# Dummy matmuls in the beginning of a two-layer cross-attention kernel

## The chip, the cores and the metric

The kernel runs on one core of a Trainium2 chip. A core has five engines with their own instruction queues: TensorE (PE: matmuls, with its weight loads shown apart as PEld), VectorE (DVE), ScalarE (ACT), GpSimd (POOL) and SyncE (SP, which here only starts DMA transfers). Each engine works through its queue in order and waits for the others by semaphores. The metric is the device time of one execution in microseconds (us), the median of the runs.

## What is computed

Two cross-attention layers, one after the other, on x (16 items, 256 rows, 320 channels) with a context of 16 x 256 x 512. There are 20 heads of 16 channels. The first layer, cut to what matters:

```python
text = context[:, :77]; ip = context[:, 77:]        # 77 text tokens, 179 image tokens
q = x @ Wq
text_out = softmax(q_h @ k_h.T * scale) @ v_h       # per head, keys and values from text
scores   = q_h @ ip_k_h.T * scale                   # per head, keys from ip
text_probs = softmax(q @ k_text.T * scale)          # over all channels, not per head
sem   = (text_probs @ text) @ ip.T * scale          # one row of image scores for all heads
ip_out = softmax(scores + 0.5 * sem) * mask @ ip_v_h
x = (text_out + ip_out) @ Wout + bout + x
```

The second layer has the same form with 252 text and 4 image tokens and a normalised semantic term per head. All arithmetic must be near f32.

## The kernel before

**Products.** PE multiplies in a rounded 32-bit format (`fp32r`), so each operand is split into a rounded high part (a cast on ACT) and a low remainder (a subtraction on DVE or POOL): `halves`. A product is then three matmuls for each 128 rows of contraction (high by high, high by low, low by high): `prod`. Results go to PSUM; a PSUM bank holds 128 x 512 f32. The general banks are called X; `bank()` hands out three of them in turn (`BANKS`, `"X": 3`), so a product waits until what stood in the bank three products earlier has been read.

**The two layers as slots.** An item's 20 heads are five groups of four, so each layer has 80 slots, numbered k. For a group, `stacks0(k)` loads by DMA a stacked query matrix `qs` and key matrix `ks` (parts Q and K: the query and key rows out of DRAM, where `queries` and `keys_out` wrote them, to `qd` and `kd`; parts T and M: the text probabilities `tph` and a Gram matrix `M` of the context), `score0` multiplies them into the S banks and takes row maxima on DVE, `maxima0` turns the maxima by a matmul with the identity `ident_r` and loads them into the stack, `turned0` multiplies again, transposed, into the T banks and takes exponentials on ACT and a factor on POOL, `attend0` multiplies by the values. `slot0(k)` lists that work for a slot, with marks (`yield 0.2`, `yield 0.6`) at which other tasks that are due are filled in.

**The beginning.** Before slot 0 nothing is there to overlap with. The loads and splits of the context, of the weights and of x stand first in the program (`all_halves`); then `begin()` runs single steps of the tasks of items 0 and 1 by hand: `k0` is the keys of both items (weights `wA` for the text keys, `wB` for the rest), `q0` the queries (split of x into `hq`, three products with `wE`), `m0t` the Gram matrix, `s0` the semantic term (products of `kb` and `q`, softmax, two transposes, products of `tph` and `M`), `v0` the values (`wC`, `wD`). `begin()` fixes the order on all five engines, the loop over slots only that of PE; the loads and splits ahead of `begin()` and, in the loop, the work of the other engines are placed by the scheduler of the framework, so that a change on PE can move them.

A line that the steps below need: `nc.vector.tensor_scalar_mul(wqt[:, 2, ...], ..., tmask[:, 3:4])` (L308) masks the low part of the last rows of `wE`, and the query products that use them come after it. `zone` is a 128 x 32 f32 tile of zeroes with a column of ones, `hsn` an f32 tile of 128 x 768 that collects attention results.

Of the kernel before, what the change touches and what calls it, by code (L numbers as in the profile page):

```python
# [49 lines left out]
def xattn2(  # L50
# [27 lines left out]
    nc = tc.nc  # L78
    f = lambda ap: ap.bitcast(F32)
    mm = nc.tensor.matmul  # L80
# [9 lines left out]
    def bank(tag="X"):  # L90
        return ps.tile([128, 512], F32, tag=tag, name=tag, bufs=BANKS[tag])
# [4 lines left out]
    def own(tag):  # L96

        n, *ring = kept[tag]
        kept[tag][0] += 1
        return ring[n % len(ring)]  # L100

    def scores(kept=False):

        s = whole if kept else ps.tile([128, 1024], F32, tag="S", name="S", bufs=1)
        return s.rearrange("p (h t) -> p h t", h=4)
# [4 lines left out]
    def buf(tag, shape, dtype=F32, bufs=1, name=None):  # L110
        if tag in ("wB", "wD", "vr", "raw"):
            return sb.tile(shape, dtype, tag=tag, name=name or tag, bufs=bufs)
        size = 1
        for d in shape[1:]:
            size *= d
        if tag not in slots:
            slots[tag] = [0, dtype] + [const_tile([128, max(size, words.get(tag, 0))], f"{tag}_{i}", dtype) for i in range(bufs)]
        n, kind, *ring = slots[tag]
        assert kind == dtype and len(ring) == bufs, tag
        slots[tag][0] += 1  # L120
        t = ring[n % bufs][: shape[0], :size]
        names = "abcd"[: len(shape) - 1]
        if len(names) > 1:
            t = t.rearrange(f"p ({' '.join(names)}) -> p {' '.join(names)}", **dict(zip(names, shape[1:])))
        return t

    def const_tile(shape, tag, dtype=F32):
        return const.tile(shape, dtype, tag=tag, name=tag)
# [7 lines left out]
    ident_r = const_tile([128, 128], "ident_r", FR)  # L136
# [6 lines left out]
    def queued(inst, *behind):  # L143

        for other in behind or [anchors.get(inst.ins.engine)]:
            if other is not None:
                tc.add_manual_dep(
                    inst.ins, other.ins.name, mybir.DependencyInfo(mybir.DependencyClass.NoSync, mybir.DependencyReason.DATA), reason="order"
                )
        return inst  # L150

    def anchor(inst):
        anchors[inst.ins.engine] = inst
        return inst
# [186 lines left out]
    zone = const_tile([128, 32], "zone")  # L341
    nc.vector.memset(zone, 0.0)
    nc.vector.memset(zone[:, 21:22], 1.0)
    hsn = const_tile([128, 3, 8, 2, 16], "hsn")
    nc.gpsimd.memset(f(buf("q", [128, 2, 3, S], FR))[64:, :, 2], 0.0)

    rn = const_tile([128, BI], "rn")
# [296 lines left out]
    def load(src, tag):  # L644
        x = buf(tag, [128, 3, S])
        dma(x, src.rearrange("(k p) t -> p k t", p=128))
        return x
# [59 lines left out]
    def stacks0(k, parts="KQTM"):  # L707
        b, g = divmod(k, NG)
        Q, K = QK[k] = qs[k % SIZES["NR"]], ks[k % SIZES["NR"]]
        for part in parts:  # L710
            if part == "K":
                dma(K[0:XROW], stack_rows(kd[0][b // 2][:, :, b % 2], g))
            elif part == "Q":
                dma(Q[0:XROW], stack_rows(get("q0", b)[1], g))
            elif g < SIZES["NR"]:
                tph, mh = get("s0", b)[1::2] if part == "T" else (None, get("m0t", b))
                if part == "T":
                    dma(Q[XROW : XROW + T0], tph[:, 0:1].to_broadcast([T0, 4, S]))
                else:
                    dma(K[XROW : XROW + T0, :, T0:], mh[:, 0:1, T0:].to_broadcast([T0, 4, S - T0]))  # L720
# [19 lines left out]
    def score0(k, t):  # L740
        Q, K = QK[k]
        if t == 0:
            maxes[k] = buf("mn", [128, 2, 2, 4], FR, bufs=2)
        mn = maxes[k]
        sp = scores(True)
        for h in range(4):
            mm(sp[:, h], Q[: XROW + T0, h, t * 128 : (t + 1) * 128], K[: XROW + T0, h], start=True, stop=True)  # L747
        nc.vector.tensor_reduce(mn[:, t, 0], sp[:, :, :T0], axis=AX.X, op=ALU.max)  # L748
        anchor(nc.vector.tensor_reduce(mn[:, t, 1], sp[:, :, T0:], axis=AX.X, op=ALU.max))  # L749

    def maxima0(k, queue=nc.scalar):
        Q, mn = QK[k][0], maxes[k]
        mp = bank()
        for t in range(2):
            mm(mp[:8, t * 128 : (t + 1) * 128], mn[:, t].rearrange("p a h -> p (a h)"), ident_r, start=True, stop=True)
        mt = buf("mt", [8, S], FR)
        nc.scalar.copy(mt, mp[:8, :S])  # L757
        for a in range(2):
            row = XROW + T0 + a
            issues[k] = queue.dma_start(f(Q[row : row + 1]), f(mt[4 * a : 4 * a + 4]))  # L760

    def turned0(k, t):

        rs = get("s0", k // NG)[2]
        Q, K = QK[k]
        for p in range(2):
            if t == 0:
                P[k, p] = buf("P", [128, 2, 2, S], bufs=SIZES["NP"])
        st = [own("T").rearrange("p (h t) -> p h t", h=2) for p in range(2)]
        for p in range(2):  # L770
            for j in range(2):
                mm(st[p][:, j], K[:KS0, 2 * p + j, t * 128 : (t + 1) * 128], Q[:KS0, 2 * p + j], start=True, stop=True)  # L772
        for p in range(2):
            pt = P[k, p][:, t]
            exp = anchor(nc.scalar.activation(pt, st[p], AF.Exp, scale=SCALE))  # L775
            if t and k + 1 in issues:
                queued(exp, issues[k + 1])
            anchor(nc.gpsimd.tensor_mul(pt, pt, rs[:, t : t + 1].to_broadcast([128, 2, S])))  # L778

    def attend0(k):  # L780
        b, g = divmod(k, NG)
        v, pv = get("v0", b), own("P")
        for vt in range(3):
            values0(k, pv, v, vt)
        settle0(b, g, pv)

    def slot0(k):
        if k > 0:
            yield lambda: maxima(k + 1)
        yield lambda: ahead(k + 2, 0)  # L790
        yield lambda: turned0(k, 0)
        yield 0.2
        if k > 0:
            yield lambda: attend0(k - 1)
        yield lambda: ahead(k + 2, 1)
        yield lambda: turned0(k, 1)
        yield lambda: stacks(k + LEAD)
        yield 0.6
        yield 1.0

# [328 lines left out]
    def step(key):  # L1129
        t = tasks[key]  # L1130
        if callable(t[2]):
            for n in t[3]:
                get(*n)
            t[2] = t[2]()
        try:
            next(t[2])
            t[1] += 1
        except StopIteration as e:
            results[key] = e.value
            del tasks[key]  # L1140

    def get(*key):
        while key not in results:
            step(key)
        return results[key]
# [27 lines left out]
    for c in range(B // 2):  # L1173
        n, k = 10 * c, [("k0", c)] if c else []
# [11 lines left out]
    for b in range(B):  # L1186
        n = NS + 5 * b
# [17 lines left out]
    def stacks(k):  # L1205
        if 0 <= k < 2 * NS:
            (stacks0 if k < NS else stacks1)(k)

    def ahead(k, t):
        if k < NS:  # L1210
            score0(k, t)
        else:
            both1(k - 2, t)

    def maxima(k):
        if k < 2 * NS:
            (maxima0 if k < NS else maxima1)(k)

    def begin():
        parts = lambda *keys: [step(key) for key in keys if key in tasks]  # L1220
        k0, q0, s0, m0, q1 = ("k0", 0), ("q0", 0), ("s0", 0), ("m0t", 0), ("q0", 1)
        parts(k0, k0, k0, q0, q0, q1, q0, q0, q0)
        get(*q0)
        get(*m0)
        parts(s0, s0, s0, s0, s0)
        stacks0(0, "M")
        stacks0(1, "M")
        parts(k0, k0, k0, s0, q1, q1, q1, q1)
        stacks0(0, "QK")
        get(*s0)  # L1230
        stacks0(0, "T")
        stacks0(1, "QKT")
        get("v0", 0)
        v1 = ("v0", 1)
        stacks0(2)
        parts(k0)
        score0(0, 0)
        parts(v1)
        score0(0, 1)
        get("m0t", 1)  # L1240
        maxima0(0, nc.sync)
        parts(v1)
        get(*v1)
        get(*q1)
        score0(1, 0)
        stacks0(3)
        score0(1, 1)
        parts(*[("s0", 1)] * 3)
        maxima0(1, nc.sync)
        parts(("s0", 1), ("s0", 1), ("k0", 1))  # L1250
        resid0.append(load(xT_d[0], "xc"))
        dma(mk, mk_d)
        dma(bo[:, 0, :], bo0_d)
        dma(bo[:, 1, :], bo1_d)
        fill(-1e-6)
# [93 lines left out]
```

## Time and profile before

| what | us |
|---|---|
| runs | 1521.59, 1528.58, 5161.13 |
| median of the runs | 1528.58 |
| the profiled execution | 1527.85 |
| its span, first to last instruction | 1526.1 |
| PE busy, share of the span | 1432.1 (94%) |
| DVE, ACT, POOL busy | 1125.5 (74%), 920.5 (60%), 1219.6 (80%) |

One run is far off the other two; the median is not moved by it. The page also cuts the span into 40 slices of 38 us and gives for each the busy share of an engine in tenths and the clock that PE was granted:

```profile
PE   6789999999999999789999999999999999999996
PEclk9899999999999998889999999999999999999997
```

PE is nearly always busy, but for the first two slices, a place in the middle where the second layer begins, and the end; in the same places the granted clock is under full. How such views are read: a group or a piece of timeline has its start and length in us, the engine, the line of the program, the operation, what it writes and reads, and in square brackets the idle time before it and what ended that. A matmul's length contains a latency that overlaps with the next, so the cost of matmuls in a row is read from start to start.

### The profile page before, as it was taken

The page shows a single profiled execution, that of the slowest core. Times are in us where ns is not written, and L with a number is a line of the kernel's source. Part 1 is how long each engine was busy: PE and PEld are TensorE (multiplying, and loading weights), DVE is VectorE, ACT ScalarE, POOL GpSimd, SP SyncE. Part 2 cuts the span into 40 slices and gives each one's busy share as a digit, 9 for nine tenths or more (in the row PEclk, how much of TensorE's full clock was granted, in tenths as well). Part 3 has the DMA queues.
Part 4 walks back from the last instruction along what each step waited for, and adds up shares of the span by engine and source line. Part 5 has one row for each costly group of instructions (what it writes and reads, how often), then busy time and mean ns, then how long its engine had stood idle before and what let it go on. Part 6 is the DMA issues. An engine that isn't in the chain of part 4 may idle for free.

```text
span 1526.1 us, 36176 instructions
## 1 busy us (share of the span) xinstructions
PE 1432.1 (94%) x12678; PEld 1158.5 (76%) x12678; DVE 1125.5 (74%) x2546; ACT 920.5 (60%) x2168; POOL 1219.6 (80%) x1583
## 2 busy tenths in 40 slices
PE   6789999999999999789999999999999999999996
PEld 6678878888888877667777777777777777777764
DVE  5467767676767677877777878887878778787884
ACT  5346565656555644556666766667756666677562
POOL 4269898989898976789678888788878788888785
PEclk9899999999999998889999999999999999999997
DMA  6766776767767664676354344444444344433311
GB/s 205 203 190 194 219 195 213 200 210 203 214 181 218 190 200 125 187 210 183 104 142 123 110 121 129 126 121 134 112 116 144 112 112 135 135 114 99 109 30 40
DMA packets 228753, 232.95 MB, mean 153 GB/s; under 512 B 38298, under 2 KB 198460, under 8 KB 228572
## 3 DMA queue, kind: packets, MB, share of 16 engines
q1 hardware_dynamic: 226364, 229.34, 52.2%
q8 instruction: 101, 1.65, 0.5%
q10 hardware_dynamic: 2208, 1.30, 0.4%
q14 instruction: 80, 0.66, 0.2%
HBM read 117.65 MB, written 77.20 MB: 128 GB/s over the span
## 4 chain that ended last, share of the span: by engine, by line
PE 67%; DMA 10%; POOL 8%; DVE 6%; ACT 3%; issue 2%; SPq 2%; ACTq 1%; POOLq 0%; DVEq 0%
PE X L946 13%; PE X L248 13%; PE X L614 6%; PE P L805 6%; PE S L747 5%; PE P L958 4%; PE P L968 4%; PE T L772 3%; PE S L903 3%; POOL wt L937 3%; PE T L897 3%; SPq L83 2%; DMA rawc<-in_cT_dram 2%; PE X L617 2%; PE X L573 2%
## 5 line engine op out<-in xcount | busy, mean ns | idle before, releaser
L778 POOL TENSOR_TENSOR P<-P,rs 128x512 f32<-128x512 f32 x320 | 408.9, 1304 | 103.1 <-ACT P L775 102.7
L937 POOL TENSOR_TENSOR wt<-P,ctb 128x512 f32<-128x512 f32 x320 | 406.4, 1293 | 57.5 <-ACT ctb L936 57.5
L946 PE MATMUL X<-ctb,gm 128*128 128x512 f32 x1120 | 301.5, 401 | 2.4 <-DVE wt L947 2.4
L775 ACT ACTIVATE P<-T 128x512 f32<-128x512 f32 x320 | 176.0, 595 | 155.9 <-PE T L772 126.0
L947 DVE TENSOR_TENSOR wt<-X,wt 128x512 f32<-128x512 f32 x320 | 217.5, 683 | 58.2 <-PE X L946 55.0
L946 PEld LDWEIGHTS X<-ctb,gm 128*128 128x128 f32 x1120 | 194.7, 189 | 41.6 <-DVE wt L947 12.0
L917 ACT ACTIVATE P<-T 128x512 f32<-128x512 f32 x320 | 174.5, 592 | 80.4 <-PE T L897 77.4
L936 ACT ACTIVATE ctb<-P 128x512 fp32r<-128x512 f32 x320 | 184.3, 626 | 12.8 <-PE X L946 9.9
L905 DVE TENSOR_REDUCE mn<-S 128x4 fp32r<-128x1008 f32 x160 | 191.2, 1195 | 0.0
L749 DVE TENSOR_REDUCE mn<-S 128x4 fp32r<-128x716 f32 x160 | 142.5, 891 | 0.0
L805 PE MATMUL P<-P,vr 128*32 128x256 f32 x1920 | 127.7, 396 | 4.5 <-POOL P L778 2.3
L747 PE MATMUL S<-ks,qs 125*128 125x256 f32 x640 | 118.2, 308 | 8.3 <-DMA qs<-tph 4.6
L747 PEld LDWEIGHTS S<-ks,qs 125*128 125x128 f32 x640 | 89.0, 195 | 43.7 <-issue 29.2
L772 PE MATMUL T<-qs,ks 127*128 127x256 f32 x640 | 106.7, 290 | 2.4 <-ACT P L775 1.3
L748 DVE TENSOR_REDUCE mn<-S 128x4 fp32r<-128x308 f32 x160 | 74.7, 467 | 34.0 <-PE S L747 33.2
L772 PEld LDWEIGHTS T<-qs,ks 127*128 127x128 f32 x640 | 90.8, 195 | 3.9 <-ACT P L775 1.7
L805 PEld LDWEIGHTS P<-P,vr 128*32 128x32 f32 x1920 | 56.7, 112 | 47.0 <-issue 7.0
L816 DVE STREAM_TRANSPOSE nt<-P 128x512 f32<-128x512 f32 x80 | 56.9, 712 | 45.3 <-PE P L805 44.3
L958 PE MATMUL P<-P,v1t 128*32 128x256 f32 x1280 | 85.7, 385 | 0.0
L968 PE MATMUL P<-wt,zone 128*32 128x256 f32 x1280 | 84.4, 379 | 0.3 <-DVE wt L947 0.3
L614 PE MATMUL X<-hq,wE 128*128 128x256 f32 x512 | 77.7, 296 | 7.2 <-ACT hq L601 3.9
L614 PE MATMUL X<-ho,wF 128*128 128x256 f32 x512 | 76.3, 292 | 7.2 <-ACT mt L757 3.7
(249 smaller groups left out, 3022.3 us busy)
## 6 DMA issues: line engine op xcount, KB each, us to landing
qd<-q SPq DMA_DIRECT2D x96, 256.0 KB
qs<-tph SPq DMA_DIRECT2D x64, 308.0 KB
rawc<-in_cT_dram SPq DMA_DIRECT2D x60, 256.0 KB
qs<-qd SPq DMA_DIRECT2D x80, 192.0 KB
ks<-kd SPq DMA_DIRECT2D x80, 192.0 KB
ks<-kd SPq DMA_DIRECT2D x160, 96.0 KB
qs<-qd SPq DMA_DIRECT2D x160, 96.0 KB
kd<-kst SPq DMA_DIRECT2D x57, 256.0 KB
```

What stands on the lines that cost most here:

```text
L248: last = mm(out, lhs(a, k), rhs(b, k), start=i == 0, stop=i == len(terms) - 1)
L614: mm(pp, w(s, k, m), a[:, t], start=i == 0, stop=i == len(terms) - 1)
L747: mm(sp[:, h], Q[: XROW + T0, h, t * 128 : (t + 1) * 128], K[: XROW + T0, h], start=True, stop=True)
L772: mm(st[p][:, j], K[:KS0, 2 * p + j, t * 128 : (t + 1) * 128], Q[:KS0, 2 * p + j], start=True, stop=True)
L775: exp = anchor(nc.scalar.activation(pt, st[p], AF.Exp, scale=SCALE))
L778: anchor(nc.gpsimd.tensor_mul(pt, pt, rs[:, t : t + 1].to_broadcast([128, 2, S])))
L805: mm(pv[32 * s : 32 * s + 32, o : o + S], v[:, vt, h : h + 32], P[k, s // 2][:, t, s % 2], start=vt < 2, stop=vt != 1,)
L905: anchor(nc.vector.tensor_reduce(maxes[k + 2][:, t], sp[:, :, :T1], axis=AX.X, op=ALU.max))
L936: nc.scalar.activation(R[k, u][:, t], P[k, u][:, t], AF.Copy, scale=0.5)
L937: anchor(nc.gpsimd.tensor_sub(W[k, u][:, t], P[k, u][:, t], f(R[k, u][:, t])))
L946: mm(yp, gm[:, gb], R[k, u][:, kt], start=i == 0, stop=i == len(blocks[n]) - 1)
L947: w1["wt"] = nc.vector.tensor_mul(W[k, u][:, n], yp, W[k, u][:, n])
```

## The change

The change adds matmuls whose results nobody reads, in six places, and a memset:

- `hsn` is set to zero by DVE at the start;
- five f32 matmuls of `zone` with the zeroes of `hsn` at the head of `begin()` (four of 256 columns, one of 128);
- a function `warm(n)`: n matmuls of the identity with itself repeated, 128 x 512, into one X bank;
- `warm(10)` before the queries of item 0, `warm(6)` before those of item 1, `warm(16)` before the first score, and `warm(7)` twice in slot 0: before the second item's transposes and before its `tph` products.

```diff
     hsn = const_tile([128, 3, 8, 2, 16], "hsn")
+    nc.vector.memset(hsn, 0.0)
...
         yield lambda: turned0(k, 0)
+        if k == 0:
+            yield lambda: warm(7)
         yield 0.2
...
         yield lambda: stacks(k + LEAD)
+        if k == 0:
+            yield lambda: warm(7)
         yield 0.6
...
+    def warm(n):
+
+        out = bank()
+        for i in range(n):
+            mm(out, ident_r, ident_r.unsqueeze(1).to_broadcast([128, 4, 128]), start=True, stop=True)
+
     def begin():
+        out = bank()
+        for m, half in ((0, slice(0, 8)), (1, slice(0, 8)), (2, slice(0, 4))):
+            rhs = hsn[:, m, half].rearrange("p f r d -> p (f r d)")
+            for i in range(2 if m < 2 else 1):
+                mm(out[:32, : rhs.shape[1]], zone, rhs, start=True, stop=True)
...
-        parts(k0, k0, k0, q0, q0, q1, q0, q0, q0)
+        parts(k0, k0, k0, q0, q0, q1)
+        warm(10)
+        parts(q0, q0, q0)
...
-        parts(k0, k0, k0, s0, q1, q1, q1, q1)
+        parts(k0, k0, k0, s0, q1)
+        warm(6)
+        parts(q1, q1, q1)
...
         parts(k0)
+        warm(16)
         score0(0, 0)
```

The scheduler also places some loads and splits of the beginning otherwise. On ACT, from the first evacuation of key products (`kst`) to the split of x (`hq`), there stands before (the names: `wB`, `wC`, `wE` are weights that are split, `raw`, `rawc` and `P` the buffers they were loaded into, `ho` the third key tile):

```order
L160 CAST kst_0_254<-X_259 128x2x77
L160 CAST wB_90<-P_1_97 128x320
L160 CAST wE_0_88<-raw_137 128x320
L160 CAST wB_91<-P_2_98 128x320
L160 CAST wC_0_172<-raw_176 128x320
L160 CAST kst_1_255<-X_275 128x2x77
L160 CAST wB_92<-P_3_99 128x320
L160 CAST wC_0_172<-rawc_0_93 128x320
L267 CAST ho_0_256<-X_291 64x2x77
L268 COPY both_0_300<-X_291 64x154
L601 CAST hq_0_307<-xq_0_133 128x512
L602 ACTIVATE hq_0_307<-xq_0_133,tmask_81 128x256
```

and now:

```order
L160 CAST kst_0_261<-X_266 128x2x77
L160 CAST wB_89<-P_0_96 128x320
L160 CAST wB_90<-P_1_97 128x320
L160 CAST kst_1_262<-X_282 128x2x77
L267 CAST ho_0_263<-X_298 64x2x77
L268 COPY both_0_307<-X_298 64x154
L602 CAST hq_0_314<-xq_0_133 128x512
L603 ACTIVATE hq_0_314<-xq_0_133,tmask_81 128x256
L160 CAST wE_0_88<-raw_137 128x320
L160 CAST wB_91<-P_2_98 128x320
L160 CAST wC_0_172<-raw_176 128x320
L160 CAST wB_92<-P_3_99 128x320
```

All three key evacuations and the split of x have moved ahead of five weight splits, which now wait behind what PE has to deliver.

On DVE the low parts follow the same way. After the split of x, up to the mask of `wE` (L308), there stands now:

```order
L604 TENSOR_TENSOR hq_0_314<-xq_0_133,hq_0_314 128x512
L605 TENSOR_TENSOR hq_0_314<-xq_0_133,hq_0_314 128x256
L163 TENSOR_TENSOR wE_0_88<-raw_137,wE_0_88 128x260
L163 TENSOR_TENSOR wE_0_88<-raw_137,wE_0_88 128x4
L163 TENSOR_TENSOR wE_0_88<-raw_137,wE_0_88 128x60
L163 TENSOR_TENSOR wB_91<-P_2_98,wB_91 128x260
L163 TENSOR_TENSOR wB_91<-P_2_98,wB_91 128x4
L163 TENSOR_TENSOR wB_91<-P_2_98,wB_91 128x60
L163 TENSOR_TENSOR wC_0_172<-raw_176,wC_0_172 128x320
```

followed by `wB_92` (three rows), `wC_0_172` and L308; before, L308 stood ahead of `wB_92` and of the split of x.

On PE, at the first score (S; `wC` and `wD` are the value products around it, `ident_r` the identity), the difference is:

```order
 L248 MATMUL X<-wD,ctb_85 128x320 x3
 L248 MATMUL X<-wD,ctb_86 128x320 x3
-L747 MATMUL S<-ks_207,qs_203 128x256 x4
+L1228 MATMUL X<-ident_r 128x512 x16
+L748 MATMUL S<-ks_207,qs_203 128x256 x4
 L248 MATMUL X<-wC_172,cta_83 128x320 x3
 L248 MATMUL X<-wC_172,cta_84 128x320 x3
```

Nothing is moved here; the sixteen stand between the values of item 0 and the score. After slot 0 the order on PE is unchanged, on SP and POOL it differs in a few places by one or two rows, and on DVE and ACT in some dozens of places of the first layer by one to seven rows.

## The prediction

> **What bounds the kernel now.** I read the windows first. Columns: stretch, length, busy time and instruction count of PE, PEld, DVE, ACT, POOL, then granted clock, DMA share, GB/s.
>
> ```profile
> 0.00:35.50 35.50, 23.05 (x112) 21.05 (x112) 22.29 (x81) 20.74 (x52) 16.75 (x25) 1.00 0.67 210
> 35.50:38.90 3.40, 3.06 (x14) 3.07 (x15) 0.42 (x1) 0.37 (x1) 1.14 (x3) 0.50 0.72 187
> 38.90:49.20 10.30, 6.70 (x48) 6.43 (x46) 1.27 (x3) 3.21 (x7) 0.23 (x1) 1.00 0.78 211
> 49.20:56.00 6.80, 5.81 (x25) 5.84 (x26) 1.81 (x4) 0.53 (x1) 0.00 (x0) 0.50 0.90 267
> 69.60:76.30 6.70, 4.76 (x22) 4.51 (x23) 5.72 (x9) 4.74 (x10) 4.95 (x4) 0.50 0.92 241
> 110.00:290.00 180.00, 175.66 (x1666) 152.47 (x1660) 125.66 (x300) 106.92 (x253) 163.03 (x158) 1.00 0.69 198
> 290.00:740.00 450.00, 412.71 (x3734) 346.14 (x3734) 322.41 (x754) 250.27 (x595) 377.72 (x384) 0.94 0.67 193
> ```
>
> From 110 to 290 us PE is busy 175.66 of 180 us: what the beginning saves reaches the end nearly one for one. The beginning is another regime: three stretches (35.5 to 38.9, 49.2 to 56.0, 69.6 to 76.3) run at half clock, 3.4, 6.8 and 6.7 us long, as if the clock were set once in 3.4 us. The first row says 1.00, but there the rate of the matmuls, from the PE timeline, is the better witness (start, length, engine, line, operation, count):
>
> ```profile
> 10.85 1.49 PE L248 MATMUL X<-cta,wA 128*128 128x156 f32 x6
> 12.13 1.49 PE L248 MATMUL X<-ctb,wA 128*128 128x156 f32 x6
> 81.42 0.79 PE L248 MATMUL X<-cta,wA 128*128 128x156 f32 x6
> 82.05 0.83 PE L248 MATMUL X<-ctb,wA 128*128 128x156 f32 x6
> 22.45 1.27 PE L617 MATMUL X<-hq,wE 128*128 128x256 f32 x5
> 35.84 3.42 PE L614 MATMUL X<-hq,wE 128*128 128x256 f32 x15 [0.97 <-POOL hq L603]
> 39.09 0.75 PE L617 MATMUL X<-hq,wE 128*128 128x256 f32 x5
> 39.68 0.28 PE L698 MATMUL X<-tph,M 77*128 77x256 f32 x1
> ```
>
> Start to start, six key products take 12.13-10.85 = 1.28 us (0.213 each) early and 0.63 us (0.105) at 81 us. The query product costs (39.09-35.84)/15 = 0.217 us at 36 us, where half clock is recorded, and (39.68-39.09)/5 = 0.118 after it; at 22.45 five take 1.27 us against 0.75. So PE is at half rate through its early work too.
>
> How much work holds the clock? Busy PE in single windows of 3.4 us laid on the same grid:
>
> ```profile
> 49.20:52.60 3.40, 2.41 (x10) 0.50 0.84 216
> 59.40:62.80 3.40, 2.02 (x15) 1.00 0.44 126
> 66.20:69.60 3.40, 1.63 (x10) 1.00 0.54 151
> ```
>
> After 2.02 us of work (59%) full clock stayed; after 1.63 us (48%) it fell. After 2.41 us (71%) it was not given back; after 3.06 us (90%, second row of all) it was. [...]
>
> **The change, part by part.** The price of a dummy, at full clock:
>
> ```profile
> 905.27 1.05 PE L968 MATMUL P<-wt,zone 128*32 128x256 f32 x16
> ```
>
> A 128x512 identity product streams twice the columns of a 128x256 one: 2x0.118 = 0.236 us (an estimate), 0.47 at half clock. The products on zeroes are f32 like this zone group: 16 records, two for each product and four products side by side, in 1.05 us, so one product takes about 0.5 us, the block of four and a half 2.3, and 4.6 at half clock. It waits for the added hsn memset, which no row shows; a POOL memset of 1024 elements takes 0.96 us (below), so 768 take about 0.7, hidden since DVE has nothing before 4.80 us. The zeroes run from 1.8 to 6.4 us against a first product at 5.18 that in any case waits for its splits until 7.02: cost 0.
>
> ```profile
> 0.88 0.96 POOL L326 MEMSET ks<- 128x1024 f32 x1
> 4.80 0.69 DVE L163 TENSOR_TENSOR cta<-rawc,cta 128x512 fp32r<-128x512 f32 x1 [3.78 <-ACT cta L160]
> 7.02 0.96 PE L248 MATMUL X<-cta,wA 128*128 128x156 f32 x3 [0.63 <-ACT wA L160]
> 14.81 0.62 DVE L163 TENSOR_TENSOR wB<-P,wB 128x260 fp32r<-128x260 f32 x3
> 15.50 0.46 ACT L160 CAST wB<-P 128x320 fp32r<-128x320 f32 x1 [0.96 <-DMA P<-in_wki_dram]
> 16.28 0.38 DVE L308 TENSOR_SCALAR wE<-wE,tmask 128x320 fp32r<-128x320 f32 x1
> 26.29 1.01 PE L670 MATMUL X<-kb,q 128*128 128x156 f32 x7 [0.21 <-DVE q L270]
> ```
>
> Term 1, up to the semantic products of item 0 at 26.29. ACT's order now has the key evacuations and the split of x ahead of the splits of wE row 2 and wB; POOL's order is as before. If PE had full clock from 10.85, the remaining 20 key products end near 10.85+20x0.105 = 13, and ACT's four evacuations and the split of x, each some 0.4 us, near 15. DVE subtracts from 14.2 on, once half of x is cast, seven groups of about 0.6 us like the wB one, before it comes to L308: 18.4 (the last wB load, landed at 15.50, is no limit then). The 14 query products that need L308 end near 21 at the latest, against 22.45+1.27 = 23.7 at half clock now: about 2.6 us early. If PE stays at half, the keys end at 15.2 as now, ACT stands idle for them, L308 slips from 16.28 to 20.8, and 14 products of 0.217 end at 23.8: 0. I expect something between. The zeroes fill a window and release the clock; but then three products at 0.105 per load of some 1.5 us are far under 48% busy, so it falls again before 10.85 and returns inside the unbroken run that follows, between 12.6 and 15. That is nearer the low end: 1.2 us. The ten identity products after the keys (2.4 to 4.7 us) end before L308 in either case: 0.
>
> Term 2, queries of item 1. Six dummies (1.4 us) fill most of the 1.71 us gap before 34.48; with the 0.4 us product there and what ran before, the window stays near 59%. Fifteen products then take 15x0.118 = 1.8 us instead of 39.09-35.84 = 3.25: 1.5 us, on the chain, since SP's row of writes to qd and then the stack loads follow them:
>
> ```profile
> 34.48 0.39 PE L614 MATMUL X<-hq,wE 128*128 128x256 f32 x1 [1.71 <-ACT hq L601]
> 44.21 5.85 DMA qs<-tph
> 50.19 1.19 PE L747 MATMUL S<-ks,qs 125*128 125x256 f32 x4 [4.59 <-DMA qs<-tph]
> 51.19 1.80 PE L248 MATMUL X<-wC,cta 128*128 128x320 f32 x6
> 54.38 1.05 PE L747 MATMUL S<-ks,qs 125*128 125x256 f32 x4
> 55.24 1.04 PE L248 MATMUL X<-cta 128*77 128x192 f32 x6
> 40.16 1.04 PE L248 MATMUL X<-wC,cta 128*128 128x320 f32 x6
> 41.92 1.04 PE L248 MATMUL X<-wD,cta 128*128 128x320 f32 x6
> ```
>
> Those transfers have room: the DMA engines are 0.78 busy from 38.9 to 49.2, 2.3 us of slack.
>
> Term 3, the first score. Sixteen dummies take 3.8 us of the 4.59 us in which PE waits for the stack; margin 0.8. Score and values then run at full clock: 12 value products 54.38-51.19 = 3.19 against 41.92-40.16 = 1.76 (1.4 saved), the two scores take half of 1.0 and of 0.86 (0.9), the token products 0.3 less. Late next is the maximum on DVE, two reductions after each score:
>
> ```profile
> L749 DVE TENSOR_REDUCE mn<-S 128x4 fp32r<-128x716 f32 x160 | 142.5, 891 | 0.0
> L748 DVE TENSOR_REDUCE mn<-S 128x4 fp32r<-128x308 f32 x160 | 74.7, 467 | 34.0 <-PE S L747 33.2
> ```
>
> Together 1.36 us, against some 1.1 us of token products behind the second score: 0.3 is given back, 2.3 us remain.
>
> Term 4, slot 0. Seven dummies (1.65 us) fit the 1.95 us gap ahead of 71.54, and seven a like gap ahead of the transposes before it. What follows, at half clock:
>
> ```profile
> 71.54 0.55 PE L698 MATMUL X<-tph,M 77*128 77x256 f32 x1 [1.95 <-DVE tph L692]
> 74.70 1.40 PE L248 MATMUL X<-cta,wA 128*128 128x156 f32 x6
> 76.95 1.50 PE L805 MATMUL P<-P,vr 128*32 128x256 f32 x24
> 74.00 1.49 DVE L163 TENSOR_TENSOR ctb<-raw,ctb 128x512 fp32r<-128x512 f32 x1 [0.21 <-ACT ctb L160]
> ```
>
> The stretch 71.54 to 74.70 would halve, but the keys behind it then wait for the last ctb split, done at 75.49, and end three products later at 75.8 instead of 76.95: 1.2 us (2.2 if that split takes 0.69 as at 4.80). The dummies each take one of three X banks; the product that needs that bank next comes two banks later, and its evacuation is done by then: 0.
>
> Sum: 1.2+1.5+2.3+1.2 = 6.2 us. The profiled execution took 1527.85 us, 0.73 under the median of 1528.58: forecast 1521.7.
>
> **The rivals.** (a) The dummies do not do what they say at the start: the gaps for x, L308 and POOL's split idle long enough that terms 1 and 2 bring 0.5 in place of 2.7. Time 1527.85-(0.5+2.3+1.2) = 1523.9. For it: L308 is late behind the new ACT order. Against: six dummies bridge the gap before 34.48. [...] (b) The clock stays up from the zeroes on, and no load holds the end: 2.6+1.5+2.5+2.2 = 8.8, 1519. Against it: between loads PE has too little to do, as term 1 says. (c) Slower: the layer's later stalls. From 290 to 740 us the clock averages 0.94, so 27 us of clock are lost there, 27/1.7 = 16 half windows. Those windows depend on where the grid falls on each stall, and every start is now shifted. Four windows more or fewer are 7 us, what separates the runs of 1521.59 and 1528.58; from four more on the gain is gone, at six (10.2 us) the time is 1527.85-6.2+10.2 = 1531.9. Nothing says the shift favours either sign.
>
> **How the numbers follow.** Forecast 0.5, (a) 0.2, (b) 0.17, (c) 0.13. The likeliest is 1521.7. The range takes (b) with 7 us of grid luck below, and most of (c) above: 1512 to 1530. Within 2% (30.6 us, about what a measurement of this kernel can tell from no change) lie all four cases, and the whole half-clock loss of the beginning, (3.4+6.8+6.7)/2 = 8.5 us, is far under that; what is left over is for causes that no row shows: faster 0.02, same 0.95, slower 0.03.
>
> **What would show it.** Right: no half-clock window at 33 to 37, 44 to 54 or 63 to 71; the query products of item 1 at 0.118; the first S product at 50.19-2.7 = 47.5; the first P product at 70.7; the rest as before. Wrong: key products still at 0.213 past 15 us and L308 past 20 (term 1), an S product that waits for dummies instead of the stack (term 3), or a total in 290 to 740 that moved by more than 6 us.

## The result and the profile after

The changed kernel takes 1515.25 us (median of 11 runs, 1510.7 to 1520.4); the kernel before took 1526.02 us beside it (median of 11). The ratio is 0.9936, with a 95% interval of 0.9917 to 0.9955, so about 10 us less (7 to 13). The forecast was 1521.7 us within 1512 to 1530, with 6.2 us to be gained. The profiled execution took 1513.42 us, its span is 1511.6 us. The time lies in the range; the gain is larger than the sum, and the traces say where it came from.

The windows of the changed kernel come first, the same stretches as before (stretch, length, busy time and count of PE, PEld, DVE, ACT, POOL, then granted clock, DMA share, GB/s):

```profile
35.50:38.90 3.40, 3.40 (x28) 3.35 (x29) 0.85 (x2) 1.48 (x4) 0.90 (x3) 1.00 0.69 151
38.90:49.20 10.30, 8.59 (x50) 7.61 (x48) 0.84 (x2) 2.10 (x4) 0.00 (x0) 1.00 0.94 248
49.20:56.00 6.80, 6.38 (x49) 6.19 (x50) 2.92 (x5) 1.43 (x4) 0.00 (x0) 1.00 0.91 282
69.60:76.30 6.70, 5.16 (x39) 3.02 (x39) 4.53 (x7) 2.62 (x6) 4.52 (x5) 0.75 0.55 110
290.00:740.00 450.00, 416.17 (x3851) 349.31 (x3850) 329.96 (x777) 258.75 (x614) 386.40 (x393) 0.97 0.68 195
```

The half clock of 35.5 to 38.9 and of 49.2 to 56.0 is gone, that of 69.6 to 76.3 is halved. Not in the sum is the last row: 0.97 for 0.94. Second, rows out of the PE timeline of the changed kernel (start, length, line, operation, count, and the wait before):

```profile
1.78 3.52 PE L1235 MATMUL X<-hsn,zone 128*32 128x256 f32 x10 [1.78 <-DVE zone L343]
11.18 1.49 PE L248 MATMUL X<-cta,wA 128*128 128x156 f32 x6
12.46 1.49 PE L248 MATMUL X<-ctb,wA 128*128 128x156 f32 x6
15.45 3.83 PE L1228 MATMUL X<-ident_r 128*128 128x512 f32 x10
20.70 1.33 PE L615 MATMUL X<-hq,wE 128*128 128x256 f32 x9 [0.61 <-DVE wE L308]
25.81 1.01 PE L671 MATMUL X<-kb,q 128*128 128x156 f32 x7 [1.18 <-DVE q L270]
35.36 2.15 PE L615 MATMUL X<-hq,wE 128*128 128x256 f32 x15 [0.96 <-POOL hq L604]
37.34 0.75 PE L618 MATMUL X<-hq,wE 128*128 128x256 f32 x5
43.69 3.80 PE L1228 MATMUL X<-ident_r 128*128 128x512 f32 x16
49.37 0.71 PE L748 MATMUL S<-ks,qs 125*128 125x256 f32 x4 [1.87 <-DMA qs<-tph]
62.23 0.65 PE L773 MATMUL T<-qs,ks 127*128 127x256 f32 x4
71.61 0.56 PE L248 MATMUL X<-ctb,wA 128*128 128x156 f32 x3 [1.12 <-DVE ctb L163]
72.60 0.47 PE L248 MATMUL X<-ctb,wA 128*128 128x156 f32 x2 [0.42 <-DVE ctb L163]
72.99 2.79 PE L810 MATMUL P<-P,vr 128*32 128x256 f32 x24
```

The key products of 11.18 still start 0.213 us apart (12.46-11.18 = 1.28 for six), the wait for L308 ends at 20.70, the queries of item 1 run at (37.34-35.36)/15 = 0.132, the sixteen dummies do not hold up the score (it waits 1.87 us more, for the stack), and the last keys wait for the split of `ctb`.

The same instruction has another start in each profile, which makes a table of leads. "T of slot n" is the first turned product of a slot (L773, L772 before).

| instruction | before | after | lead |
|---|---|---|---|
| last semantic products, item 0 | 26.29 | 25.81 | 0.48 |
| last queries, item 1 | 39.09 | 37.34 | 1.75 |
| first S | 50.19 | 49.37 | 0.82 |
| T of slot 0 | 65.35 | 62.23 | 3.12 |
| first P | 76.95 | 72.99 | 3.96 |
| T of slot 10 | 152.18 | 153.40 | -1.22 |
| T of slot 30 | 306.56 | 305.01 | 1.55 |
| T of slot 79, the last of the first layer | 710.93 | 697.88 | 13.05 |
| end of the span | 1526.1 | 1511.6 | 14.5 |

In this pair the lead of 4 us at the first P is used up by slot 10: the changed kernel has two half windows there (stretches of 3.4 us at half clock, from 72.9 and from 107.0 us), the kernel before none between 76.5 and 298 us. The lead comes to 13 us between slots 30 and 79. The windows of that stretch and of what is left, before and then after:

```profile
306.60:710.90 404.30, 370.48 (x3366) 312.82 (x3364) 292.36 (x683) 221.43 (x528) 338.19 (x340) 0.95 0.67 192
710.90:1526.10 815.20, 788.60 (x6971) 606.10 (x6969) 636.42 (x1370) 530.50 (x1234) 655.89 (x1018) 0.99 0.40 115
```

```profile
305.00:697.90 392.90, 362.51 (x3367) 307.06 (x3365) 289.40 (x682) 221.65 (x527) 339.95 (x340) 0.97 0.69 198
697.90:1511.60 813.70, 787.39 (x6971) 605.24 (x6969) 636.98 (x1370) 530.49 (x1234) 656.37 (x1018) 0.99 0.40 115
```

The same matmuls (3366, but for one at the edge) take 404.3 and 392.9 us; the second layer takes 815.2 and 813.7. In the traces' records of the clock all distances between two changes are whole multiples of 3.413 us (29 of 29 before, 21 of 21 after); by them the stretch has 13 half windows before and 8 after. Each takes 1.7 us of clock, if PE is busy in it: 22.2 against 13.7 us.

### The profile page after: what moved, and what is told of

It reads as the page before. It is cut to its first block, busy times and chain, and to the rows that moved or that the text cites. A ratio compares the mean times of both kernels' runs of the same rounds, so it can differ in the third digit from the quotient of the medians.

```text
span 1511.6 us, 36290 instructions
## 1 busy us (share of the span) xinstructions
PE 1431.3 (95%) x12734; PEld 1153.5 (76%) x12734; DVE 1124.0 (74%) x2547; ACT 920.1 (61%) x2168; POOL 1222.4 (81%) x1583
## 4 chain that ended last, share of the span: by engine, by line
PE 73%; DMA 7%; POOL 7%; DVE 5%; ACT 3%; issue 2%; SPq 1%; ACTq 1%; POOLq 0%; DVEq 0%
PE X L951 15%; PE X L248 13%; PE X L615 7%; PE P L810 6%; PE S L748 5%; PE P L963 5%; PE P L973 4%; PE T L773 4%; PE T L902 3%; PE S L908 3%; POOL P L779 3%; PE X L618 2%; PE X L258 2%; PE X L574 2%; POOL wt L942 2%
## 5 line engine op out<-in xcount | busy, mean ns | idle before, releaser
L941 ACT ACTIVATE ctb<-P 128x512 fp32r<-128x512 f32 x320 | 184.2, 626 | 12.1 <-PE X L951 9.0
L773 PE MATMUL T<-qs,ks 127*128 127x256 f32 x640 | 106.7, 289 | 2.3 <-DMA qs<-mt 1.5
L773 PEld LDWEIGHTS T<-qs,ks 127*128 127x128 f32 x640 | 90.2, 194 | 4.7 <-ACT P L776 1.9
L248 PE MATMUL X<-wC,cta 128*128 128x324 f32 (+1 forms) x480 | 79.4, 312 | 0.3 <-DVE kst L270 0.3
```

Source lines behind the costliest of these rows:

```text
L248: last = mm(out, lhs(a, k), rhs(b, k), start=i == 0, stop=i == len(terms) - 1)
L941: nc.scalar.activation(R[k, u][:, t], P[k, u][:, t], AF.Copy, scale=0.5)
```

## Experiments

Two questions: what the dummies bring and what the moved rows bring, and within the dummies, what the start brings and what the rest. "The rest" is the dummies before the queries of item 1, before the first score and in slot 0 (terms 2 to 4). A pair of profiles can't answer this: runs of one kernel differ by some 10 us, so each kernel was timed in five rounds against the kernel before.

To part dummies and rows, the order of ACT, DVE, POOL and SP was fixed, row by row, by a dependency that carries no wait, from a table of positions:

```diff
-    with tc.manual_schedule(engines=PINNED | {getattr(mybir.EngineType, e) for e in ("SP", "Activation", "DVE", "Pool")}):
+    with tc.manual_schedule(engines=PINNED):
         begin()
...
+    for engine, packed in ORDERS.items():
...
+        row = [mine[n + d] for n, d in enumerate(moves)]
+        for one, two in zip(row, row[1:]):
+            tc.add_manual_dep(two, one.name, ..., reason="order")
```

**Order alone, and dummies alone.** The first is the kernel before with that edit and the order of after; the second is the changed kernel with it and the order of before.

> The kernel before, without any dummy, with ACT, DVE, POOL and SP put in exactly the order that they have in the changed kernel. Theory D (the dummies bring the whole of the 10.8 us, the moved rows nothing): 0 us against before, within 3. Theory O (the moved rows of the beginning and of the first layer bring a part): 3 to 6 us faster. Theory M (the new order suits only a PE at full clock, since ACT stands idle for the key products): 1 to 4 us slower.

> The changed kernel with all its dummies and the memset, with ACT, DVE, POOL and SP kept in the order of the kernel before. Theory D: 10 to 11 us faster than before, as the change. Theory O: 5 to 7 us faster, what terms 2, 3 and 4 of the prediction add up to. Theory M: more than the change brings, 12 us or more.

Measured: 1520.82 us (ratio 0.9978, 0.9957 to 0.9999) and 1518.41 us (0.9952, 0.9928 to 0.9976). Read plainly, 3.4 us for the order and 7.3 for the dummies, which happens to be the whole gain. The control below overturns that reading.

**Start alone, and the rest alone, in the order of after.** Third and fourth kernel. The edit of the fourth is shown; the third leaves out the other four calls of `warm` and keeps these.

```diff
-        for m, half in ((0, slice(0, 8)), (1, slice(0, 8)), (2, slice(0, 4))):
...
-                mm(out[:32, : rhs.shape[1]], zone, rhs, start=True, stop=True)
...
-        warm(10)
```

> Only the five products on zeroes and the ten identity products after the keys are kept; the order of the other engines is that of the changed kernel. The prediction's term 1: 1.2 us faster than before (0 to 2.6), with the half-clock stretches at the queries of item 1, the first score and slot 0 as in before. If the start carries the surplus over the forecast (theory S): 5 us or more.

> Only the six, the sixteen and twice seven identity products are kept, in the order of the changed kernel. The prediction's terms 2 to 4: 5 us faster than before. Theory S: the same 5 us, and the rest of the 10.8 is missing. If these dummies carry nearly all of it: 9 to 11 us.

Measured: 1524.05 us (0.9999, 0.9974 to 1.0024) and 1516.76 us (0.9946, 0.9924 to 0.9968). The rest looked like everything and the start like nothing.

**Which rows of the order?** The edit is that of the first kernel with another table of positions, cut in two: the first 60 rows of ACT and SP and 150 of DVE in the new order and all else in the old one (fifth kernel), and the reverse (sixth).

> The kernel before, without any dummy; of the new order only the beginning (the first 60 rows of ACT and SP, the first 150 of DVE; 22, 22 and 41 rows stand elsewhere than before), all that is later as before. The whole new order without dummies brought 3.4 us (ratio 0.9978, 0.9957 to 0.9999). Theory H (the loads and splits of the beginning carry it): about -3.4 us, and the first S product about 2 us earlier than 50.19. Theory L (the small swaps among the later splits carry it, since they decide how long the stalls from 300 to 650 us last): about 0. Theory N (the order brings nothing, and the 3.4 us were scatter): about 0, and e6 about 0 as well.

> The kernel before, without any dummy; the beginning in the order of before, and all that is later on ACT, DVE, POOL and SP in the new order (43, 73, 30 and 13 rows stand elsewhere). Theory H: about 0. Theory L: about -3.4 us. Theory N: about 0.

Measured: 1518.03 us (0.9953, 0.9932 to 0.9973) and 1519.65 us (0.9956, 0.9932 to 0.9981). Two halves worth 7 us each hardly make a whole of 3.4, though the intervals overlap; none of the three theories has this. Something that all fixed kernels have in common may be at work.

**The rest in the old order, and more dummies.** The seventh kernel is that of "the rest alone" with the order of before; the eighth is that of "the rest alone" in the new order with three more places, shown here.

```diff
+        if k == 73:
+            yield lambda: warm(14)
         if k > 0:
             yield lambda: maxima(k + 1)
...
+        if k == 4:
+            yield lambda: warm(8)
         if k > 0:
             yield lambda: attend0(k - 1)
...
         yield 0.6
+        if k == 69:
+            yield lambda: warm(18)
         yield 1.0
```

> The order of before on ACT, DVE, POOL and SP, and of the dummies only those before the queries of item 1, before the first score and in slot 0 (no zeroes, none before the queries of item 0). The prediction's terms 2, 3 and 4 give 1.5+2.3+1.2 = 5.0 us: 1521. If the dummies at the start add 1.2 us as term 1 has it, this kernel is 1.2 us slower than the one with all dummies in the old order (1518.4, 7.3 us under before); if they cost something, as the comparison of the two kernels without them suggests (1516.8 against 1515.3 with, 1524.1 with them alone against 1520.8 without), it is level with it or faster. First P product some 4 us under 76.95 in either case.

> The new order, the dummies before the queries of item 1, before the first score and in slot 0, and three more places where every trace so far shows PE idle: 8 before the values of slot 4 (idle 1.5 to 2.5 us), 18 before the transposes that wait 4.6 to 7.1 us in slot 69, 14 before the maxima that wait 3.7 to 4.6 us in slot 73. Theory C (the time lost there is half clock after the stall, one or two windows of 3.4 us each at half): 1.7 to 3.4 us at each place less, 5 to 8 us under the 1516.8 of the same kernel without them, so 1509 to 1512; no half clock right behind 104, 630 and 652 us. Rival F (the clock before the stall, or the dummies' own time where the wait is shorter, eats it): 1515 to 1519. Rival D (the layer there is bound by DVE and DMA, PE only waits elsewhere): 1516, with the half clock gone and the waits longer.

Measured: 1513.66 us (six runs, 0.9917, 0.9886 to 0.9947) and 1517.45 us (0.9942, 0.9921 to 0.9964). The seventh kernel lies 12.4 us under before, the second, which has the dummies at the start as well and the same old order, only 7.5: by the expectation the start costs something there, though the two intervals overlap. The dummies of the eighth kernel did their work. Here is its PE timeline in the slots 4 and 73:

```profile
104.65 2.09 PE L1234 MATMUL X<-ident_r 128*128 128x512 f32 x8
106.77 1.50 PE L816 MATMUL P<-P,vr 128*32 128x256 f32 x24
...
650.38 3.38 PE L1234 MATMUL X<-ident_r 128*128 128x512 f32 x14
653.59 0.22 PE L756 MATMUL X<-ident_r,mn 128*8 128x128 f32 x1
654.55 0.23 PE L756 MATMUL X<-ident_r,mn 128*8 128x128 f32 x1 [0.74 <-DVE mn L750]
```

The values of slot 4 take 1.50 us and not 2.79 as in the fourth kernel, and the maxima of slot 73 wait 0.74 us behind the dummies instead of 3.66. The window around the two late places:

```profile
612.00:665.00 53.00, 45.74 (x405) 34.60 (x405) 43.33 (x98) 26.93 (x63) 41.82 (x46) 0.94 0.67 182
```

and the same window of the kernel without the three places:

```profile
612.00:665.00 53.00, 40.47 (x369) 30.65 (x370) 42.06 (x95) 26.33 (x62) 41.73 (x46) 0.84 0.64 173
```

The clock rises from 0.84 to 0.94, but DVE is busy 43.33 of 53 us beside it and POOL 41.82. The total, 1517.45 against 1516.76, did not fall by the 5 to 8 us of theory C; it lies where rivals F and D have it. From slot 30 to 79 this kernel has 6 half windows against 9 of the fourth, but takes 387.6 against 383.1 us apart from them: what the clock gave was lost beside it. Whether to the dummies' own time (F) or to the other engines (D) stays open.

**The control.** The kernel before, with nothing moved and nothing added, only its own order fixed; and the same for the changed kernel.

> A control. The kernel before, no dummy, no row moved: only the means by which the other experiments fix an order is in it (a dependency without a wait from each row of ACT, DVE, POOL and SP to the next). The rows of all five engines are the same, but the places at which some of them wait are not: 219 rows of PE have another set of waits (the row whose wait a later row inherits), on the other engines five. Theory W (these moved waits are what made every kernel with a fixed order faster: 3.4, 7.2 and 6.7 us for the whole order, its beginning alone and its rest alone, which do not add up): 4 to 7 us under before, and then the order itself is worth about nothing. Theory O (the order brings it): 1526, as before.

> The same control on the changed kernel: all dummies, its own order, fixed. Theory W, if the gain is additive: 1509 to 1511, 4 to 6 us under the changed kernel's 1515.3; if what the moved waits bring lies in the same stalls as what the dummies bring: 1515. Theory O: 1515.3.

Measured: 1515.73 us (0.9932, 0.9908 to 0.9955) and 1514.67 us (0.9923, 0.9898 to 0.9948). The fixing alone, without a dummy and without a moved row, is worth as much as the whole change, more than the 4 to 7 us of theory W; on the changed kernel it brings next to nothing more. So the order itself is not what made the fixed kernels faster. Most of it is not the clock: over all runs the mean granted clock of the first control is 0.975, against 0.973 of the kernel before, which is under 3 us. Its windows, from slot 30 to slot 79 and from there to the end:

```profile
308.20:714.00 405.80, 370.15 (x3365) 312.74 (x3364) 289.30 (x681) 222.21 (x528) 339.11 (x340) 0.94 0.67 191
714.00:1519.10 805.10, 781.15 (x6971) 604.78 (x6969) 636.10 (x1370) 529.11 (x1234) 654.77 (x1018) 0.99 0.41 116
```

The first stretch is as long as before (405.8 against 404.3). The second layer takes 805.1 us in place of 815.2, with the same 6971 matmuls: PE is 7.45 us less busy and 2.65 us less idle. Part of this is clock, which the rounded 0.99 hides: by the clock's record 3.6 half windows lie in it against 6.7, so up to 5.3 us. The rest is not. From slot 10 to slot 60 of the second layer, by the first turned product of each, both have full clock all the time; here is the kernel before, and then the control:

```profile
816.50:1311.90 495.40, 491.03 (x4384) 380.83 (x4382) 394.61 (x851) 332.99 (x780) 408.21 (x631) 1.00 0.43 123
817.20:1306.60 489.40, 487.78 (x4386) 382.02 (x4384) 394.67 (x850) 332.07 (x781) 407.42 (x631) 1.00 0.44 125
```

That is 6.0 us. Over all profiles this stretch takes 489.3 to 493.9 us in the kernels of fixed order and 492.1 to 495.4 in those of free order. The rows are the same (one memset on DVE at the start changes places with its neighbour), the places of the waits on PE are not; that the waits are the cause is likely but not shown.

**The free kernels.** The last two have no fixed order, so the scheduler places their rows: the changed kernel with the rest alone (the edit of the fourth kernel), and with the start alone.

> The changed kernel without the zeroes and without the dummies before the queries of item 0; the order is left to the scheduler. It comes out almost as before (9 rows of ACT, 17 of DVE, 6 of POOL and 5 of SP differ), so that the moved rows of the change hang on the two left out. If the gain is the prediction's terms 2, 3 and 4 and nothing else: 1526.0-5.0 = 1521. If these dummies carry the whole change: 1515 to 1516. If the start and its moved rows carry the surplus: 1519 to 1522.

> The changed kernel with only the zeroes and the dummies before the queries of item 0; the order is left to the scheduler and comes out nearly as in the change (20 rows of ACT, 35 of DVE, 13 of POOL, 7 of SP differ from it; 55, 85, 17 and 28 from before). The prediction's term 1, with moved rows at nothing: 1526.0-1.2 = 1524.8. If the start or its moved rows carry the surplus: 1519 to 1522. If they cost something: over 1526.

Measured: 1521.61 us (0.9967, 0.9943 to 0.9991) and 1518.87 us (0.9957, 0.9928 to 0.9986). The rest alone brings 5.1 us where the terms 2 to 4 say 5.0. The start alone, with the rows that move with it, brings 7.9 where term 1 says 1.2: 1518.87 lies just below the 1519 to 1522 that were expected if the start or its rows carry the surplus. Here is the window of the kernel with the rest alone from the first record of full clock on:

```profile
23.10:105.00 81.90, 69.86 (x524) 61.61 (x527) 44.48 (x102) 36.41 (x93) 29.68 (x30) 1.00 0.73 209
```

No half window is left in 82 us.

**All twelve, with the second layer taken out.** The change has nothing in the second layer, and in the four kernels of free order it takes 815.2, 813.7, 813.9 and 814.5 us. The fixed ones have 805.1 to 813.9. So I take from each difference of medians the difference of the second layers. That is an estimate, since each kernel has one profile, and not always a typical one: that of kernel 9 is the slowest of its twelve runs, those of 1 and 3 are the fastest. The second layer also has half windows of its own, 3.5 to 6.7 of them up to the end of the span.

| kernel | median, us | against before of the same runs | second layer, us | first layer against before |
|---|---|---|---|---|
| order alone (1) | 1520.82 | -5.1 | 808.3 | +1.8 |
| head of the order (5) | 1518.03 | -8.0 | 807.9 | -0.7 |
| later order (6) | 1519.65 | -6.4 | 811.6 | -2.8 |
| before, fixed (9) | 1515.73 | -11.0 | 805.1 | -0.9 |
| rest, new order (4) | 1516.76 | -9.1 | 809.6 | -3.5 |
| rest, old order (7) | 1513.66 | -12.4 | 807.7 | -4.9 |
| rest, free (11) | 1521.61 | -5.1 | 813.9 | -3.8 |
| rest and three places (8) | 1517.45 | -8.6 | 811.8 | -5.2 |
| start, new order (3) | 1524.05 | -1.9 | 812.9 | +0.4 |
| start, free (12) | 1518.87 | -7.9 | 814.5 | -7.2 |
| all, old order (2) | 1518.41 | -7.5 | 813.9 | -6.2 |
| all, fixed (10) | 1514.67 | -12.1 | 811.9 | -8.8 |
| the change | 1515.25 | -10.8 | 813.7 | -9.3 |

Each number is uncertain by 3 to 5 us (the ratios' intervals reach 0.0019 to 0.0031 to each side), the last column by more. The means of the groups are steadier: without dummies -0.7, whatever the order; with the rest -4.1 (three kernels); with all -8.1. The two with the start alone contradict each other. No experiment clearly beats the changed kernel: the lowest ratio, 0.9917 (0.9886 to 0.9947), overlaps its 0.9936.

## Why the prediction was right, and where it was not

**Term 1 (1.2 us): 0.5 in the pair, with two errors inside.** Over the profiles, the last semantic product starts at a mean of 26.4 us with zeroes (five kernels) and 27.2 without (nine). The first steps came as forecast: the zeroes release the clock (its first record, full, begins at 4.64 us), and it falls again (half from 8.05 us). Then the text had the clock return "between 12.6 and 15", in the run of key products, and the ten identity products cost and bring nothing. Here are the changed kernel's windows on the grid of its clock:

```profile
1.22:4.64 3.42, 2.85 (x7) 1.25 (x8) 0.49 (x2) 1.43 (x3) 3.38 (x5) 1.00 0.77 217
4.64:8.05 3.41, 2.27 (x10) 1.28 (x8) 2.47 (x8) 1.59 (x5) 3.41 (x5) 1.00 0.94 304
8.05:11.46 3.41, 2.42 (x8) 2.01 (x8) 2.80 (x11) 2.87 (x7) 3.35 (x5) 0.50 0.95 310
11.46:14.88 3.42, 3.42 (x18) 3.42 (x17) 3.13 (x17) 1.26 (x4) 1.91 (x5) 0.50 1.00 348
14.88:18.29 3.41, 3.41 (x11) 2.83 (x11) 2.56 (x12) 2.57 (x8) 1.43 (x2) 0.50 0.07 24
18.29:21.70 3.41, 2.80 (x20) 2.42 (x19) 2.76 (x12) 1.08 (x3) 3.23 (x2) 1.00 0.66 212
```

From 11.46 to 14.88 PE is busy all the time with key products, and the clock is not given; it is given at 18.29, after the window that holds most of the ten identity products. The kernel with the start alone in the fixed order shows the same, with the zeroes split over two windows and no release by them:

```profile
11.17:14.58 3.41, 3.41 (x18) 3.41 (x18) 2.94 (x16) 1.66 (x5) 2.03 (x6) 1.00 1.00 360
14.58:18.00 3.42, 3.42 (x10) 2.65 (x10) 3.33 (x13) 3.25 (x10) 1.98 (x3) 1.00 0.09 31
18.00:21.40 3.40, 2.84 (x21) 2.54 (x20) 2.39 (x11) 0.90 (x4) 0.00 (x0) 1.00 0.80 257
```

(Its clock column reads 1.00 because its first record is at 18.0.) So busy time was the wrong measure. What decides instead no run tests by itself. The row from 11.46 shows the weight loads busy for all of 3.42 us, and by an estimate from the measured costs a key product of 156 columns streams for 156/256 of 0.118 us = 0.072 at full clock but takes 0.105, so only about 68% of its time would be streaming; that this is the measure is a guess. The prediction's 71% that was not enough before is a share of busy time, so it sets no bound for this one. In the changed kernel the zeroes released the clock with PE busy for 2.85 of 3.42 us, and the window of key products did not with 3.42 of 3.42, so the busy time of the profile does not decide it. The slip of L308 (PE waits for it until 20.70; the text had 20.8 at worst) and the missing gain at the keys came as the low bound had it, and with the keys at 0.213 up to 15.45 us the prediction's own sign against term 1 is there. The ten dummies, where the text had written 0, seem to be what gave the queries of item 0 the clock: it is back at 16.5 to 20.1 us in the five profiles that have them and at 23.0 to 26.2 in the nine that have not.

**Term 2 (1.5 us): 1.27**, the growth of the lead from 0.48 to 1.75.

**Term 3 (2.3 us): 2.30 after the first S, and -0.93 before it.** From the first S to T of slot 0 it takes 62.23-49.37 = 12.86 in place of 65.35-50.19 = 15.16, exactly the term. But the first S came at 49.37 and not at 47.5: the step that gave the transfers 2.3 us of room was wrong. They had been 0.78 busy; moved together they are 0.94 busy (second row of the windows after). The last transfer of the stack starts 1.72 us earlier (42.49 for 44.21) but takes 6.74 us in place of 5.85, and so the stack lands late by most of what term 2 had gained. No dummy held up the score, the other way it could have failed.

**Term 4 (1.2 us): 0.84**, from 3.12 to 3.96, and the limit is the one named, the split of `ctb` (1.12 and 0.42 us of waiting). The values behind it then run in a new half window, 24 products in 2.79 us.

**The X banks and the moved rows (0).** For the rows this holds as far as the runs tell: -0.7 us in the mean of four kernels without dummies; and of the pairs with fixed order that differ in nothing else, the new order is slower than the old one by 5.9 us (1 and 9) and 3.3 (4 and 7) and faster by 4.6 (10 and 2). The X banks were not tried apart.

**The sum.** At the first P the terms make 3.96 of the 6.2 us, and this pair flatters them: over the profiles the first P starts at a mean of 75.3 us without dummies (five kernels), 72.6 with the rest (four) and 73.8 with all (three), so 1.5 to 2.7 us earlier; in the pair it came at 72.99, not at the 70.7 that was forecast. Then the step failed that carried the terms to the end "nearly one for one" and left 290 to 740 as before. By the prediction's own criterion, a total there that moves by more than 6 us, it was wrong: from slot 30 to slot 79 it moved by 11.5. In all kernels the lead at slot 30 is small: a mean of 305.8 us without dummies, 303.0 with the rest (three kernels), 303.5 with all. What follows is rival (c)'s mechanism with the other sign. Without the clock lost, slots 30 to 79 take 379 to 385 us in all thirteen kernels that have no added dummies there; most of the differences are half windows: 9 to 14 of them in the five kernels without dummies, 9 to 11 with the rest, 7 to 9 in the five with zeroes. That is shown as an account of these traces, one of each kernel.

That a kernel which begins with zeroes loses fewer windows there is not shown beyond them. The clock of every run is on record, and its means are 0.973 to 0.976 without dummies, 0.972 and 0.975 with the start alone, 0.979 to 0.983 with the rest and 0.978 to 0.979 with all. (Where the zeroes release the clock its record takes in two or three half windows of the first 20 us that the others lack: up to 0.003.) So in the means it is the rest that keeps the clock, and the start adds nothing clear to it. The times say the same where the order is fixed and only the start differs: 1.9 us under before with it against 5.1 without (kernels 3 and 1), 7.5 against 12.4 (2 and 7), 12.1 against 9.1 (10 and 4). In the free kernels, where rows and waits move along with it, it goes with 7.9 us (12) and with 5.7 (the change against 11). Each of these differences is uncertain by some 5 us.

So the forecast held with a sum of about the right size for terms 2 to 4 (5.0, against 5.1 in the free kernel, 4.1 by the table and 2.7 at the first P) and with some 4 us (8.1-4.1 by the table) where term 1 has 1.2. In the pair they came not at the start (0.5) but later, and whether the zeroes, the ten dummies, the moved rows or the moved waits bring them is open. That the time fell into the range is therefore partly luck. Of the 6.4 us between 1521.7 and 1515.25, 1.8 are the base: the forecast went out from a single execution of 1527.85, and the median of before came to 1526.02. Rival (a) is right for term 1 (0.5) and wrong for term 2; (b), a clock that stays up from the zeroes on, is refuted by the rows above.

## What to carry to other kernels

Dummies before a stall that recurs at one place cleared the half clock behind it here (granted clock 1.00 for 0.50 from 35.5 to 38.9 and from 49.2 to 56.0 us), and where matmuls stand behind them the gain came out as summed from rows (2.30 us for 2.3 after the first S); three more places in the layer raised the clock as well (0.94 for 0.84 from 612 to 665 us) and gained nothing (1517.45 against 1516.76 us). The transfers that moved with the dummies had less room than their DMA share suggested (0.78 busy became 0.94, and 0.93 us were lost). In the changed kernel the clock was full from 18.29 us, behind a window with most of the ten products of 512 columns (3.41 us busy), and still half from 14.88 us, behind one full of 156-column products (3.42 us busy). An experiment that fixes an order needs a control in which nothing else is changed: here the control moved the time by as much as the change. Where the runs of one kernel scatter by 10 us, one pair of profiles shows where, and only medians of many kernels show how much.

## What the runs showed of the hardware beyond that

- The grid of the clock, 3.413 us wide, lies elsewhere from profile to profile: its changes fall 0.93 us behind a multiple of it in the third kernel, 1.22 in the changed one, 1.39 in the kernel before and 3.03 in the tenth. The zeroes (3.52 us long in the changed kernel, 3.85 in the second, 4.04 in the third) released the clock in the changed kernel (full from 4.64 to 8.05 us), the second (half only from 8.7 us) and the tenth (full from 6.44 to 9.85 us); in the third they did not, where they are split over two windows with PE busy for 2.56 and 3.21 us.
- The kernel before with its own order of rows, fixed by dependencies that carry no wait, took 489.4 in place of 495.4 us from slot 10 to 60 of the second layer, at full clock in both. Half of it is busy time of PE (487.78 against 491.03), so no idle gap shows it.
- A dummy of 512 columns takes 0.229 us at full clock, from start to start ((653.59-650.38)/14), a little under the 0.236 estimated from one of 256.
